# Experts of two tiles in the two halves of the array, keys ahead of exponentials, sums on VectorE

## The chip, the cores and the metric

The kernel runs on one core of one Trainium2 chip. The metric is the device time of one execution in microseconds (us). The engines of a core work side by side and meet at semaphores: TensorE (PE, matrix products; PEld is its loading of weights), VectorE (DVE), ScalarE (ACT), GpSimd (POOL) and SyncE (SP), whose queue issues the DMA transfers. Sums of matrix products land in PSUM, everything else of a tile lies in SBUF. All numbers of this kernel are float32.

## The reference

One decoder layer on x of 32 x 64 rows of 512 numbers (2048 rows), with three residual additions:

```
x = x + attention(layernorm(x))                    # 32 heads of 128, biases, RMS norm of q and k, softmax
x = x + cross_attention(layernorm(x), ctx)         # blocks of 64 rows of x against 64 rows of ctx
x = x + experts(layernorm(x))
```

The cross-attention takes, for each of the 32 blocks, x as a 64 x 512 matrix (64 channels): `q = Wq x`, `k = Wk ctx`, `v = Wv ctx`, `energy = q^T k / 8`, a softmax over the 128 columns of ctx, and `Wskip x + v attention^T`.

The experts are a router with bias vectors only:

```
logits  = x @ router_weight.T + router_bias        # 64 experts
scores  = softmax(logits)
w, idx  = top_k(scores, 8)
w_dense = zeros(2048, 64) with w at idx
out     = x * sum(w) + w_dense @ expert_bias       # expert_bias: 64 x 512
```

So what an expert adds to a row is its weight times a bias row: the mixture `w_dense @ expert_bias` is a product whose contraction is only 64 long.

## The kernel before

The 2048 rows are 16 tiles of 128 rows, taken as 8 pairs (`NPAIR`, L25). The attention proper fills the span up to about 1380 us; the change touches nothing there. What follows is the output stage.

**Products.** For each pair of tiles the attention's result (`a`, loaded by `load_mixed`, L818) is multiplied with the output weights. Pair 0 uses `plain_out` (L850 and on, with `chunks`, L832, as the inner loop). Pairs 1 to 7 use `strassen_out` (L884): a Strassen scheme of seven products of half size, `product(i, a)` at L904, each from 16 float32 products of 128x128 by 128x256 (L837), with sums and differences of blocks of `a` (128 x 2048) between them: L961, L962, L968, L975 in pairs 1 to 6, L920, L921, L922, L925 in pair 7, which has its own order of products (2, 1, 6, 5, 3, 4, 7). Pairs 1 to 6 take 2, 4, 1, 5, 7, 6, 3. L957, L960, L989 and others add a product to the residual x, which `load_residual` brought in (L176 load, L825 adds the output bias).

**Tails beside the products.** `chunks` yields after every four products (L845), so a pair of seven products has 28 steps, and after each of them the main loop (L1436 to L1438) calls `advance()`, which moves the tails of the pair before by one step. A tail is what remains of a tile after the attention: `after_attention` (L1105) runs `cross_attention` (L994) and then `experts` (L1060). `yield n` in a tail means that it sits out n steps and goes on in the one after. The second tile of a pair starts three steps after the first one (L1107). The steps on PE of a tail are the keys and values `kv` (L1003, L1004), the energies `e` (L1013, in the two row halves of the array), the turned probabilities `pt_x` (L249), the result `py_x` (L1048, L1050), the turned normalised rows `pt_f` (L249), the router `pl` (L1069), the turned weights `pw` (L1096), and the mixture `pm` (L1101). Between them stand the layernorm on DVE and POOL (L225, L226, L229, L230, L239), `kvs` copied by ACT (L1007), the softmax (L1024 maxima and L1026 on DVE, eight exponentials L1030 on ACT, L1039 and L1040 on DVE), the top-8 on DVE (L1075 to L1093), and the output (L1102 adds the mixture, L1103 stores the tile by SP).

For the mixture the weights of a tile are put into the first 64 columns of a 128-column tile whose rest is zero (`wds`, L1420), turned by PE, and multiplied with a bias table whose rows 64 to 127 are zero (`eb_sb`, L1419 to L1423). The tail of the first tile of a pair ends in step 27, that of the second one in the next pair's product 2.

**What sets the order.** PE executes in the order of the program text. The instructions of DVE, ACT and POOL in the output stage are ordered by a tile scheduler when the kernel is built (the order by hand ends at `ordered.close()`, L1399). SP issues DMAs in order. PSUM buffers come from three pools: `ps_a` with three buffers (`py`, `py_x`, `pm`), `ps_t` with two (`pt`, `pw`) and `ps_s` with three (`kv`, `e`, `pl`). The residual tiles x come from `xpool` with four buffers: x of a pair takes the buffers of the pair two before it, so its load waits for that tile's output to have been stored. The last pair's tiles (14 and 15) run their tails with no products of a further pair beside them.

Of the kernel before, what the change touches and what calls it, by code (L numbers as in the profile page):

```python
# [8 lines left out]
F32 = mybir.dt.float32  # L9
AF = mybir.ActivationFunctionType  # L10
ALU = mybir.AluOpType
AX = mybir.AxisListType

P = 128
NB, SEQ, D = 32, 64, 512
NT = NB * SEQ // P
# [12 lines left out]
NEXP = 64  # L29
# [12 lines left out]
def decoder_layer(  # L42
# [23 lines left out]
    nc = tc.nc  # L66
# [9 lines left out]
    ps_a = ctx.enter_context(tc.tile_pool(name="ps_a", bufs=3, space=bass.MemoryType.PSUM))  # L76
# [138 lines left out]
    def load(to, what):  # L215

        tc.keep_in_program_order(nc.sync.dma_start(out=to, in_=what))
# [666 lines left out]
    def strassen_out(pair, right, done, a12=None):  # L884


        ta, tb = 2 * pair, 2 * pair + 1

        def beside(what):
            return work.tile([P, BLK], F32, tag=what[:3], name=f"{what}_{pair}")  # L890

        if a12 is None:
            a12 = load_mixed(ta, 1, beside("a12"))
            a22 = load_mixed(tb, 1, block(f"a22_{pair}"))
        else:
            a22 = load_mixed(tb, 1, beside("a12"))
        a11 = load_mixed(ta, 0, beside("a11"))
        a21 = load_mixed(
            tb, 0, work.tile([P, BLK], F32, tag="a21", name=f"a21_{pair}", bufs=1)
        )  # L900
        xa, xb = load_residual(ta), load_residual(tb)
        la, ra, lb, rb_ = (xt[:, bass.ts(n, DH)] for xt in (xa, xb) for n in range(2))

        def product(i, a):  # L904
            py = out_block(f"{i}_{pair}")
            yield from chunks(py, [(a, right[i])])
            return py

        def part(what):
            return work.tile([P, DH], F32, tag=what, name=f"{what}_{pair}", bufs=1)  # L910

        def add(to, what):
            nc.gpsimd.tensor_tensor(to, to, what, ALU.add)

        if pair == NPAIR - 1:

            s1, s2 = (
                beside(what).rearrange("p (g n) -> p g n", n=P) for what in ("a12_s1", "a11_s2")
            )
            nc.vector.tensor_tensor(s1, a21, a22, ALU.add)  # L920
            nc.vector.tensor_tensor(s2, s1, a11, ALU.subtract)  # L921
            nc.gpsimd.tensor_tensor(a21, a11, a21, ALU.subtract)  # L922
            py = yield from product(2, a12)
            nc.vector.tensor_tensor(la, la, py, ALU.add)
            nc.vector.tensor_tensor(a12, a12, s2, ALU.subtract)  # L925
            yield
            py = yield from product(1, a11)
            p1 = part("p1")
            nc.scalar.copy(p1, py)
            add(la, p1)  # L930
            yield
            py = yield from product(6, s2)
            nc.vector.tensor_tensor(p1, py, p1, ALU.add)
            add(ra, p1)
            add(lb, p1)
            add(rb_, p1)
            yield
            py = yield from product(5, s1)
            p5 = part("p5")
            nc.scalar.copy(p5, py)  # L940
            add(ra, p5)
            add(rb_, p5)
            yield
            py = yield from product(3, a12)
            nc.vector.tensor_tensor(ra, ra, py, ALU.add)
            done(ta, xa)
            yield
            py = yield from product(4, a22)
            nc.vector.tensor_tensor(lb, lb, py, ALU.add)
            yield  # L950
            py = yield from product(7, a21)
            nc.vector.tensor_tensor(lb, lb, py, ALU.add)
            nc.vector.tensor_tensor(rb_, rb_, py, ALU.add)
            done(tb, xb)
            return
        py = yield from product(2, a12)
        nc.vector.tensor_tensor(la, la, py, ALU.add)  # L957
        yield
        py = yield from product(4, a22)
        nc.vector.tensor_tensor(lb, lb, py, ALU.add)  # L960
        nc.gpsimd.tensor_tensor(a22, a21, a22, ALU.add)  # L961
        nc.gpsimd.tensor_tensor(a21, a11, a21, ALU.subtract)  # L962
        yield
        py = yield from product(1, a11)
        p1 = part("p1")
        nc.scalar.copy(p1, py)
        add(la, p1)
        nc.vector.tensor_tensor(a11, a22, a11, ALU.subtract)  # L968
        yield
        py = yield from product(5, a22)  # L970
        p5 = part("p5")
        nc.scalar.copy(p5, py)
        add(ra, p5)
        add(rb_, p5)
        nc.vector.tensor_tensor(a12, a12, a11, ALU.subtract)  # L975
        yield
        py = yield from product(7, a21)
        p17 = part("p17")
        nc.vector.tensor_tensor(p17, py, p1, ALU.add)
        yield  # L980
        py = yield from product(6, a11)
        nc.vector.tensor_tensor(p1, py, p1, ALU.add)
        nc.vector.tensor_tensor(p17, py, p17, ALU.add)
        add(ra, p1)
        add(lb, p17)
        add(rb_, p17)
        yield
        py = yield from product(3, a12)
        nc.vector.tensor_tensor(ra, ra, py, ALU.add)  # L989
        yield  # L990
        done(ta, xa)
        done(tb, xb)

    def cross_attention(t, xt):  # L994


        name = f"x{t}"
# [7 lines left out]

        kvs = work.tile([P, 2, MCTX], F32, tag="kvs", name=f"kvs_{t}")
        nc.scalar.copy(kvs, kv)  # L1007
        yield 1
        halves = [slice(b * SEQ, (b + 1) * SEQ) for b in range(2)]
        e = [ps_s.tile([P, 4, MCTX], F32, tag="ps", name=f"e{b}_{name}") for b in range(2)]  # L1010
        for c in range(4):
# [45 lines left out]
            )  # L1057
        nc.vector.tensor_tensor(xt, xt, py, ALU.add)

    def experts(t, xt):  # L1060
        name = f"f{t}"
        xn = layernorm(xt, name)
        yield 4
        ft = work.tile([P, KC, P], F32, tag="ft", name=f"ft_{name}", bufs=1)
        nc.scalar.copy(ft, transposed(xn.rearrange("p (kc k) -> p kc k", k=P), name))
        yield 1
        pl = ps_s.tile([P, NEXP], F32, tag="ps", name=f"pl_{name}")
        for kc in range(KC):
            nc.tensor.matmul(  # L1069
                pl, ft[:, kc, :], rwt[:, kc, :], start=kc == 0, stop=kc == KC - 1  # L1070
            )
        lg = work.tile([P, NEXP], F32, tag="lg", name=f"lg_{name}")
        nc.vector.tensor_tensor(lg, pl, rb_b, ALU.add)
        top = small.tile([P, 8], F32, tag="top", name=f"top_{name}")
        nc.vector.max(top, lg)  # L1075
        neg = small.tile([P, 1], F32, tag="neg", name=f"neg_{name}")
        nc.vector.tensor_scalar(neg, top[:, 0:1], -1.0, None, ALU.mult)
        ex = work.tile([P, NEXP], F32, tag="ex", name=f"ex_{name}")
        den = small.tile([P, 1], F32, tag="den", name=f"den_{name}")
        nc.scalar.activation(ex, lg, AF.Exp, bias=neg, accum_out=den)  # L1080
        inv = small.tile([P, 1], F32, tag="inv1", name=f"inv1_{name}")
        nc.vector.reciprocal(inv, den)

        rest = work.tile([P, NEXP], F32, tag="rest", name=f"rest_{name}")
        nc.vector.match_replace(rest, top, lg, -3e38)
        chosen = work.tile([P, NEXP], F32, tag="chosen", name=f"chosen_{name}")
        nc.vector.tensor_tensor(chosen, lg, rest, ALU.not_equal)
        wd = wds[:, t % 2, 0:NEXP]
        nc.vector.scalar_tensor_tensor(wd, ex, inv, chosen, ALU.mult, ALU.mult)
        ws = small.tile([P, 1], F32, tag="ws", name=f"ws_{name}")  # L1090
        nc.vector.tensor_reduce(ws, wd, AX.X, ALU.add)

        nc.vector.scalar_tensor_tensor(xt, xn, ws, xt, ALU.mult, ALU.add)  # L1093
        yield 4
        pw = ps_t.tile([P, P], F32, tag="pt", name=f"pw_{name}")
        nc.tensor.transpose(pw, wds[:, t % 2, :], ident)  # L1096
        wt = work.tile([P, P], F32, tag="wt", name=f"wt_{name}")
        nc.scalar.copy(wt, pw)
        yield 1
        pm = ps_a.tile([P, D], F32, tag="pa", name=f"pm_{name}")  # L1100
        nc.tensor.matmul(pm, wt, eb_sb, start=True, stop=True)  # L1101
        nc.vector.tensor_tensor(xt, xt, pm, ALU.add)  # L1102
        nc.sync.dma_start(out=out_flat[bass.ts(t, P), :], in_=xt)  # L1103

    def after_attention(t, xt):  # L1105
        if t % 2 and t < NT - 1:
            yield 2  # L1107
        yield from cross_attention(t, xt)
        yield from experts(t, xt)


# [305 lines left out]
    load(rb_b, rb.partition_broadcast(P))  # L1417

    eb_sb = work.tile([P, D], F32, tag="eb", name="eb_sb", bufs=1)  # L1419
    wds = work.tile([P, 2, P], F32, tag="wds", name="wds", bufs=1)  # L1420
    nc.gpsimd.memset(eb_sb[NEXP:P, :], 0.0)
    nc.gpsimd.memset(wds, 0.0)
    load(eb_sb[0:NEXP, :], eb)  # L1423
    for _ in range(4):
        next(outs[1])

# [65 lines left out]
```

## Time and profile before

| what | us |
|---|---|
| median of 3 runs | 1933.31 (1930.85 to 1934.56) |
| the profiled execution's own time | 1932.7 |
| its span | 1930.9 |
| PE busy | 1887.6 (98%) |
| DVE busy | 1228.4 (64%) |
| POOL busy | 1044.3 (54%) |
| ACT busy | 646.8 (33%) |
| granted TensorE clock, mean | 0.993 |

How to read it: the span is from the first to the last instruction that the profiler saw; the execution's own time lies 1.8 us above it. Busy times of different engines overlap. A row of the timeline has the start in us from the span's beginning, the time to the last end of the merged instructions, engine, line, operation, what is written and read, the count, and in brackets how long the engine stood idle ahead of it and what released it. A row of the groups has the count after x, then total busy us and mean ns of one, then the idle time before them and its releasers. Idle time counts only on the engine that sets the end. Matmuls are pipelined, so a group's mean duration is longer than the distance between two starts.

### The profile page before, as it was taken

The numbers are of one execution on the slowest core, as the hardware profiler recorded it, in microseconds if no ns is written. First come the engines' busy times: TensorE is split into PE (matmuls) and PEld (weight loads), VectorE is DVE, ScalarE is ACT, GpSimd is POOL, SyncE is SP. The second block draws the span as 40 slices with busy tenths as digits, with TensorE's granted clock in tenths as the row PEclk, the third lists the DMA queues.
The fourth block names the chain that finished last, engine by engine and source line by source line (L and its number), as shares of the span: only waits on it lengthen the run. The fifth ranks groups of instructions, "written<-read, shape, count | busy, mean of one in ns | idle before, by whom it ended". The sixth has DMA issues, their size and how long they took to land.

```text
span 1930.9 us, 40526 instructions
## 1 busy us (share of the span) xinstructions
PE 1887.6 (98%) x16877; PEld 1622.2 (84%) x16877; DVE 1228.4 (64%) x2024; ACT 646.8 (33%) x1579; POOL 1044.3 (54%) x812
## 2 busy tenths in 40 slices
PE   9999999999999999999999999999998999999997
PEld 8888888888888888888888888888886888888874
DVE  7867777676667659666666666666454545554554
ACT  2343344344333443344333434433311202221122
POOL 5856666665667539665666666565234323332320
PEclk9999999999999999999999999999998999999998
DMA  4244334334433343334433333444932231223100
GB/s 138 67 134 142 121 126 129 110 105 131 133 111 110 107 140 107 99 101 131 133 110 111 110 100 100 130 134 137 301 127 86 90 111 67 71 88 112 49 20 23
DMA packets 164568, 214.92 MB, mean 111 GB/s; under 512 B 10144, under 2 KB 135136, under 8 KB 160288
## 3 DMA queue, kind: packets, MB, share of 16 engines
q1 hardware_dynamic: 163200, 211.24, 34.1%
q8 instruction: 133, 2.18, 0.5%
q10 hardware_dynamic: 1184, 1.08, 0.2%
q14 instruction: 51, 0.42, 0.1%
HBM read 171.92 MB, written 40.37 MB: 110 GB/s over the span
## 4 chain that ended last, share of the span: by engine, by line
PE 76%; DVE 12%; POOL 7%; issue 3%; DMA 1%; ACT 1%; SPq 0%; POOLq 0%; DVEq 0%; ACTq 0%
PE p_w L655 24%; PE py L837 19%; PE va L387 7%; PE vb L387 6%; POOL qk L734 5%; PE ms_w L779 3%; PE s L555 3%; PE o L592 3%; DVE qk L666 3%; DVE qk L679 3%; DVE qk L544 1%; PE pt_p L249 1%; PE pa L445 1%; DVE sums L262 1%; PE py_x L1050 1%
## 5 line engine op out<-in xcount | busy, mean ns | idle before, releaser
L655 PE MATMUL p_w<-x,w 128*128 128x256 f32 x2940 | 723.9, 383 | 8.6 <-DVE qk L666 8.0
L655 PEld LDWEIGHTS p_w<-x,w 128*128 128x128 f32 x2940 | 521.2, 190 | 70.7 <-DVE qk L666 13.1
L666 DVE TENSOR_TENSOR qk<-p_w,qk 128x512 f32<-128x512 f32 x360 | 213.0, 600 | 135.0 <-PE p_w L655 99.1
L356 ACT ACTIVATE sq<-qk 128x512 f32<-128x512 f32 x256 | 158.1, 629 | 400.2 <-POOL qk L734 225.4
L387 PEld LDWEIGHTS va<-w,x 128*128 128x128 f32 x2048 | 263.6, 191 | 30.5 <-ACT v L403 20.6
L387 PE MATMUL va<-w,x 128*128 128x128 f32 x2048 | 276.1, 278 | 2.1 <-ACT v L403 2.1
L837 PE MATMUL py<-wo,a 128*128 128x256 f32 x1152 | 262.5, 381 | 0.0
L679 DVE TENSOR_TENSOR qk<-p_w,qk 128x512 f32<-128x512 f32 x360 | 220.1, 620 | 57.4 <-PE p_w L655 53.9
L120 POOL TENSOR_TENSOR w<-w 128x768 f32<-128x768 f32 x126 | 244.5, 1951 | 2.4
L837 PEld LDWEIGHTS py<-wo,a 128*128 128x128 f32 x1152 | 213.9, 190 | 35.6 <-issue 7.3
L265 POOL TENSOR_TENSOR prob<-prob,inv 128x512 f32<-128x512 f32 x64 | 75.3, 1177 | 294.9 <-DVE inv L264 291.7
L542 POOL TENSOR_TENSOR qk<-qk,rs 128x512 f32<-128x512 f32 x128 | 172.4, 1347 | 113.1 <-DMA rs<-row_w 92.9
L387 PEld LDWEIGHTS vb<-w,x 128*128 128x128 f32 x1536 | 201.4, 192 | 9.7
L387 PE MATMUL vb<-w,x 128*128 128x128 f32 x1536 | 202.4, 275 | 0.0
L403 ACT COPY v<-va 128x256 f32<-128x256 f32 x256 | 94.8, 370 | 308.9 <-PE va L387 308.7
L544 DVE SCALAR_TENSOR_TENSOR qk<-qk,gqk,rs 128x512 f32<-128x512 f32 x128 | 173.4, 1355 | 11.1 <-DMA rs<-row_w 10.0
L837 PE MATMUL py<-wo_t,a 128*128 128x256 f32 x608 | 144.3, 389 | 0.0
L837 PEld LDWEIGHTS py<-wo_t,a 128*128 128x128 f32 x608 | 116.1, 195 | 16.9 <-issue 0.8
L734 POOL TENSOR_TENSOR qk<-qk 128x512 f32<-128x512 f32 x60 | 90.7, 1511 | 61.1 <-DVE qk L679 58.7
L257 DVE TENSOR_REDUCE mx<-s 128x8 f32<-128x512 f32 x64 | 44.1, 689 | 106.8 <-PE s L555 106.8
L407 DVE TENSOR_TENSOR v<-vb,v 128x256 f32<-128x256 f32 x192 | 80.8, 421 | 45.6 <-PE vb L387 27.0
L607 ACT ACTIVATE ot<-o,bvt 128x256 f32<-128x256 f32 x256 | 99.2, 469 | 2.2 <-PE o L592 2.2
(182 smaller groups left out, 2198.2 us busy)
## 6 DMA issues: line engine op xcount, KB each, us to landing
rs<-row_w SPq DMA_DIRECT2D x120, 512.0 KB
mixed<-ot SPq DMA_DIRECT2D x64, 512.0 KB
a<-mixed SPq DMA_DIRECT2D x32, 1024.0 KB
w<-in_wq_dram SPq DMA_DIRECT2D x64, 256.0 KB
w<-in_wk_dram SPq DMA_DIRECT2D x62, 256.0 KB
w<-in_wv_dram SPq DMA_DIRECT2D x62, 256.0 KB
wo<-in_wo_dram SPq DMA_DIRECT2D x8, 1024.0 KB
x<-in_x_dram SPq DMA_DIRECT2D x20, 256.0 KB
```

What stands on the lines that cost most here:

```text
L120: on.tensor_tensor(*(it.rearrange("p c j d -> p (c j) d") for it in (out, a, b)), ALU.subtract)
L356: nc.scalar.activation(sq, of, AF.Square)
L387: nc.tensor.matmul(to[:, j, :], left[i][:, c, j, :], right[i][:, c, 2, :], start=first and j == 0 and c == 0, stop=c == 1, skip_group_chec ...
L403: nc.scalar.copy(self.v[h, ab], what)
L542: nc.gpsimd.tensor_tensor(k, k, rk, ALU.mult)
L544: lambda: nc.vector.scalar_tensor_tensor(q, q, gqk, rq, ALU.mult, ALU.mult)
L607: nc.scalar.activation(ot[:, h, :, b * SEQ : (b + 1) * SEQ], o[b][:, h, :, :], AF.Identity, bias=bvt[:, hg * HG + h : hg * HG + h + 1],)
L655: nc.tensor.matmul(bank[:, s, :], self.w.inner[o][i], inner_x[self.half, o][i], start=first and s == 0, stop=True, skip_group_check=True,)
L666: nc.vector.tensor_tensor(to(t, j), bank, add(t, j), ALU.add)
L679: nc.vector.tensor_tensor(to(t, j), bank, to(t, j), ALU.add)
L734: on.tensor_tensor(qk[to], qk[to], qk[what], ALU.add)
L837: nc.tensor.matmul(py, a[:, g, :], b[g // KH][:, g % KH, :], start=n == 0 and g == 0, stop=n == last and g == NHG - 1,)
```

## The change

Three things are changed.

**Experts.** The weights of both tiles of a pair go into one tile `wds` of 128 columns, 64 for each. The first tile's `experts` ends after its top-8 and leaves its weights and its x in `chosen_by`; the second tile's takes them up, turns both tiles' weights at once, and makes two mixture products, each of 64 rows: rows 0 to 63 for the first tile, 64 to 127 for the second. The bias table lies in both halves of `eb_sb`, loaded twice, and the two zero fills are gone. Both adds and both stores follow there, in the second tile's last step. Tiles 14 and 15 (`alone`) each keep a turn and a product of their own, over 64 rows. The last `yield 4` of `experts` and its first one become `yield 3`.

**Keys.** The second tile of a pair starts its tail one step after the first one's instead of three (`yield 0` in place of `yield 2`), and four steps instead of two lie from its keys to its energies (`apart`). In the built program its copy of keys and values (L1007 before) stands on ACT ahead of the first tile's eight exponentials; before, it stood behind them.

**Sums.** L961 and L962 (pairs 1 to 6) and L922 (pair 7), differences and sums of 128 x 2048 numbers, go from POOL to DVE; L962 also moves behind a `yield`.

```diff
@@ strassen_out, pair 7
-            nc.gpsimd.tensor_tensor(a21, a11, a21, ALU.subtract)
+            nc.vector.tensor_tensor(a21, a11, a21, ALU.subtract)
@@ strassen_out, pairs 1 to 6
         py = yield from product(4, a22)
         nc.vector.tensor_tensor(lb, lb, py, ALU.add)
-        nc.gpsimd.tensor_tensor(a22, a21, a22, ALU.add)
-        nc.gpsimd.tensor_tensor(a21, a11, a21, ALU.subtract)
+        nc.vector.tensor_tensor(a22, a21, a22, ALU.add)
         yield
+        nc.vector.tensor_tensor(a21, a11, a21, ALU.subtract)
         py = yield from product(1, a11)
@@ cross_attention
-    def cross_attention(t, xt):
+    def cross_attention(t, xt, apart):
...
         nc.scalar.copy(kvs, kv)
-        yield 1
+        yield apart
@@ experts
+    chosen_by = {}
+
     def experts(t, xt):
         name = f"f{t}"
         xn = layernorm(xt, name)
-        yield 4
+        yield 3
...
-        wd = wds[:, t % 2, 0:NEXP]
+        alone = t >= NT - 2
+        side = 0 if alone else t % 2
+        if side:
+            wds, other = chosen_by.pop(t - 1)
+        else:
+            wds = work.tile([P, 2, NEXP], F32, tag="wds", name=f"wds_{name}")
+        wd = wds[:, side, :]
...
-        yield 4
+        if not alone and not side:
+            chosen_by[t] = wds, xt
+            return
+        yield 3
+        n = NEXP if alone else 2 * NEXP
         pw = ps_t.tile([P, P], F32, tag="pt", name=f"pw_{name}")
-        nc.tensor.transpose(pw, wds[:, t % 2, :], ident)
+        nc.tensor.transpose(pw[0:n, :], wds.rearrange("p a e -> p (a e)")[:, 0:n], ident)
         wt = work.tile([P, P], F32, tag="wt", name=f"wt_{name}")
-        nc.scalar.copy(wt, pw)
+        nc.scalar.copy(wt[0:n, :], pw[0:n, :])
         yield 1
-        pm = ps_a.tile([P, D], F32, tag="pa", name=f"pm_{name}")
-        nc.tensor.matmul(pm, wt, eb_sb, start=True, stop=True)
-        nc.vector.tensor_tensor(xt, xt, pm, ALU.add)
-        nc.sync.dma_start(out=out_flat[bass.ts(t, P), :], in_=xt)
+        both = [(t, xt)] if alone else [(t - 1, other), (t, xt)]
+        pms = [ps_a.tile([P, D], F32, tag="pa", name=f"pm{i}_{name}") for i in range(len(both))]
+        for i, pm in enumerate(pms):
+            rows = slice(i * NEXP, (i + 1) * NEXP)
+            nc.tensor.matmul(pm, wt[rows, :], eb_sb[rows, :], start=True, stop=True)
+        for (at, it), pm in zip(both, pms):
+            nc.vector.tensor_tensor(it, it, pm, ALU.add)
+            nc.sync.dma_start(out=out_flat[bass.ts(at, P), :], in_=it)
@@ after_attention
-        if t % 2 and t < NT - 1:
-            yield 2
-        yield from cross_attention(t, xt)
+        second = t % 2 and t < NT - 1
+        if second:
+            yield 0
+        yield from cross_attention(t, xt, 3 if second else 1)
         yield from experts(t, xt)
@@ setup of the output stage
-    wds = work.tile([P, 2, P], F32, tag="wds", name="wds", bufs=1)
-    nc.gpsimd.memset(eb_sb[NEXP:P, :], 0.0)
-    nc.gpsimd.memset(wds, 0.0)
-    load(eb_sb[0:NEXP, :], eb)
+    for half in range(2):
+        load(eb_sb[half * NEXP : (half + 1) * NEXP, :], eb)
```

In the changed kernel's lines, the mixture's add of L1102 stands at L1121, and the store of L1103 behind it.

## The prediction

> **What bounds the kernel now.** First the page's busy shares and its row of granted clock, then the busy time by stretch of the output stage, which is all that the change touches, then the order in time where TensorE (PE) stands still.
>
> ```profile
> PE 1887.6 (98%) x16877; PEld 1622.2 (84%) x16877; DVE 1228.4 (64%) x2024; ACT 646.8 (33%) x1579; POOL 1044.3 (54%) x812
> ...
> PEclk9999999999999999999999999999998999999998
> ```
> PE works 98% of the span, so only shorter PE work or one of its 43 us of idle time can pay. The clock falls in two slices, around 1450 and at the very end.
>
> ```profile
> 1450.80:1538.30 87.50, 80.36 (x409) 65.52 (x408) 39.48 (x78) 15.88 (x68) 27.72 (x24) 0.94 0.28 94
> ...
> 1645.26:1707.52 62.26, 62.26 (x324) 51.33 (x323) 32.11 (x61) 11.81 (x48) 18.99 (x18) 1.00 0.26 87
> ...
> 1832.04:1895.90 63.86, 60.36 (x328) 49.99 (x327) 33.90 (x69) 14.60 (x64) 15.02 (x19) 1.00 0.06 20
> 1895.90:1930.90 35.00, 20.88 (x85) 10.98 (x83) 16.57 (x45) 8.35 (x30) 2.71 (x6) 0.77 0.08 30
> ```
> Columns: length, then busy time of PE, weight loads, VectorE (DVE), ScalarE (ACT), GpSimd (POOL), granted clock, DMA share, GB/s. A middle pair (1645 to 1707, pairs 3 to 6 are alike) has no PE gap at all, DVE half idle: there only PE instructions count. Pair 1 (first row), pair 7 (third) and the end have gaps.
>
> ```profile
> 1479.41 0.41 ACT L1007 COPY kvs<-kv 128x256 f32<-128x256 f32 x1
> ...
> 1479.88 1.16 PE L1013 MATMUL e_x<-kvs,xn_x 64*128 64x128 f32 x16 [1.71 <-ACT kvs L1007]
> ...
> 1480.97 5.41 PE L837 MATMUL py<-wo_t,a 128*128 128x256 f32 x16
> ...
> 1831.58 4.51 POOL L922 TENSOR_TENSOR a<-a,a 128x2048 f32<-128x2048 f32 x1 [8.14 <-PE pw_f L1096]
> ...
> 1831.97 6.28 DVE L921 TENSOR_TENSOR a_s<-a_s,a 128x2048 f32<-128x2048 f32 x1
> ...
> 1841.21 1.16 PE L1013 MATMUL e_x<-kvs,xn_x 64*128 64x128 f32 x16 [1.58 <-DVE xn_x L239]
> ...
> 1850.12 1.16 PE L1013 MATMUL e_x<-kvs,xn_x 64*128 64x128 f32 x16 [1.92 <-ACT kvs L1007]
> ```
> Two gaps (1.71 and 1.92) have one cause: tile B's key copy stands on ACT behind tile A's eight exponentials. The third (1.58) is A's layernorm, held on DVE by L921, which took 6.28 us while POOL's L922 ran beside it.
>
> **The change, part by part.** I call T0 the start of a pair's product 2; A and B are the two tiles of the pair before, whose tails run beside the products.
>
> *Keys ahead.* B's key product goes one step behind A's and its ACT copy ahead of A's exponentials, so both key waits go: 1.71 in pair 1 and 1.92 in pair 7. After the first gap the 16 records of 1480.97 last 5.41 us; at full rate 16 take 3.62 (the same row kind at 1844.58), so half rate cost about 1.7 more. The Trainium skill ("TensorE: Matmul & The Clock Gate", Part 1) says that PE drops to half rate when a window of about 3.4 us ends largely idle, and that the window runs free. The row is 1.71 us of gap followed by half rate, while 1.58 and 1.92 were followed by none. By the rule alone a short gap is luck and nothing more than 1.71 is sure; by the row 3.4 comes back. I take the row: with the gap gone there is nothing to trip on. Pair 1: 3.4 (1.7 to 3.4).
>
> *Sums on VectorE.* L961, L962 and L922 leave POOL:
>
> ```profile
> L961 POOL TENSOR_TENSOR a<-a,a 128x2048 f32<-128x2048 f32 x4 | 18.2, 4552 | 12.7 <-PE py L837 12.7
> L962 POOL TENSOR_TENSOR a<-a,a 128x2048 f32<-128x2048 f32 x4 | 18.1, 4527 | 0.3
> L1101 PE MATMUL pm_f<-eb_sb,wt_f 128*128 128x512 f32 x28 | 16.2, 664 | 0.4 <-ACT wt_f L1098 0.4
> ...
> L975 DVE TENSOR_TENSOR a<-a,a 128x2048 f32<-128x2048 f32 x4 | 9.2, 2292 | 0.1
> ```
> On DVE each costs 2.29, so 4.6 more per pair against some 30 idle: nothing in pairs 1 to 6, covered by that idle time. Product 5 needs L961 at T0+25.7 and it is done near 21.9; were that cover gone, each us late would be one us of PE. In pair 7 DVE carries L920, L921, L922 in a row, 6.9, without POOL beside it, against 2.28 + 6.28 before; A's normalised x comes near T0+11.4 (both mixture adds now stand ahead of it too), PE is ready near 10.9. So the 1.58 gap shrinks to about 0.6, and product 1 waits 0.3 for its buffer. Pair 7: 1.58 + 1.92 − 0.9 = 2.6 (1.0 to 3.5).
>
> *Experts side by side.* Per pair one transpose instead of two (0.11 on PE), and two mixture products of 64 rows in the two row halves instead of two of 128. A full one holds PE for 0.86 (it begins at 1647.93 in that pair, the next product at 1648.79), so 1.72 a pair. No half-array product of 512 columns is in the trace; the nearest is L1013: 16 records of 64 rows, begun in pairs a few ns apart, hold PE for 1.09, where 16 in a row at the same 0.107 would be 1.71. That is eight pairs at 0.107, plus 0.2 for entering and leaving. Upper bound: no overlap, 1.72. Lower: full overlap, 0.86. I take 0.86 + 0.19 = 1.05, by that row. Saved: 0.67 + 0.11 = 0.78 a pair. The rule that speaks against it: the skill's "TensorEngine Tiling (Array Packing)", Gotcha 1, says that different row tiles cannot use one PSUM bank at the same time. In the built program the two results lie in different buffers for pairs 3 to 7, but pair 2's (tiles 0 and 1) get the same one, so the second product waits for VectorE's add of the first (L1121 after, L1102 before), itself behind A's maxima: 0.86 + 1.0 wait + 0.86 + 0.19 for the mode, less 0.11, against 1.72. By the row alone pair 2 would gain 0.78; by the rule it loses 1.1. I take the loss. So 5 × 0.78 − 1.1 = 2.8 (between 5 × 0.11 − 1.1 and 4.7).
> The bias table is loaded twice: one more 128 KB issue on SP (0.33) and two memsets fewer on POOL, at nothing, since PE has four steps of product 2 in that time.
>
> *What is late next.* Both outputs now leave behind the mixture step of product 2, and A's add stands on DVE behind both layernorms. The next x of this buffer waits for the output:
>
> ```profile
> 1643.82 0.34 SPq L1103 DMA_DIRECT2D out_dram<-x  x1
> 1647.59 0.33 SPq L176 DMA_DIRECT2D x<-in_x_dram  x1
> ```
>
> ```profile
> 1650.43 1.27 POOL L825 TENSOR_TENSOR x<-x,bo_b 128x512 f32<-128x512 f32 x1 [3.97 <-DMA x<-in_x_dram]
> ```
>
> ```profile
> 1651.73 0.42 DVE L957 TENSOR_TENSOR x<-x,py 128x256 f32<-128x256 f32 x1 [2.05 <-POOL x L825]
> ...
> 1653.98 1.29 DVE L1024 TENSOR_REDUCE mx_x<-e_x 128x4 f32<-128x512 f32 x2 [1.83 <-PE e_x L1013]
> ```
> Before, the output goes at T0+1.1 (T0 is 1642.75 here), the load is issued 3.77 later, its bias begins 2.84 after that, L957 ends at T0+9.4. After: layernorms to 4.9, A's add to 5.6, output issued at 5.65, load 2.1 to 3.77 later (both spacings occur), bias done at 11.9 to 13.5, L957 at 12.3 to 13.9. On DVE, A's maxima are queued behind L957; ACT's exponentials wait for them, and B's second score tile takes the buffer of A's first. From maxima to the first four exponentials done are 3.0 us, so the buffer is free at 15.3 to 16.9, and PE wants it at 16.86 (1659.6 here). Cover: 0 to 1.6 us. I charge 0.2 for each of pairs 3 to 6 (0 to 0.5): 0.8.
>
> *End.* Tiles 14 and 15 keep their own products, now half-array ones. The last mixture of pair 7's first tile moves out from between two products of tile 15's chain (about 1.0 there at half clock), and one add of 0.69 moves ahead of tile 15's layernorm: 0.3 saved, ±1 for the clock.
>
> **Sum**: 3.4 + 2.6 + 2.8 − 0.8 + 0.3 = 8.3. The profiled execution's own time is 1932.7 (span 1930.9, 1.8 around it), so 1924.4; it lies 0.6 below the median of the runs, so the forecast is 1925.0.
>
> **Rivals.**
> 1. *Late x (slower).* L957 holds A's maxima, and PE stalls before B's scores in each of pairs 3 to 6. It begins when L957 ends past T0+13.9. For: the cover is near nothing at the long spacing, two loads and two outputs now stand close on SP, and a gap can bring half rate (1.7). Against: SP and DVE are more idle than not, and the short spacing leaves 1.6. At 2 us late with half rate, 3.7 × 4 = 14.8 in place of 0.8: a loss of 5.7, 1939. It cancels all gain at 2.3 us per pair.
> 2. *No overlap in the halves.* L1013's pairs speak against it; for it, that the longest row seen so is 128 columns. The products stay at 1.72: 5 × 0.67 less, gain 5.0, 1928.3.
> 3. *The waits only move.* PE is ahead at the same places for another reason (B's layernorm on DVE, half rate from an earlier gap at 1458, the longer sums in pair 7), pairs 1 and 7 give 2 instead of 6: with the overlap as forecast 1929 to 1930, with more stalls 1932. For: 43 us of gaps have several waits ending together. Against: in the gaps named the next waiter is over 1 us earlier.
>
> **How the numbers follow.** What this kernel's measurement can tell from no change is about 0.2%, 3.9 us: faster means below 1929.4, slower above 1937.2. Chances: forecast 0.55 (1922 to 1928), no overlap 0.12 (faster), waits move 0.18 (0.14 of it within 0.2%), late x 0.15 (0.13 slower, the rest within). Faster 0.71, same 0.16, slower 0.13. The range for 8 in 10 is 1920 to 1937: below, stalls of nothing and a better end; above, the late x at half its price.
>
> **What would show it.** Right: the L1013 gaps of 1.71 and 1.92 gone, full rate after 1481; the mixture pair at about 1.05 in pairs 3 to 7 with starts together; pair 2's second one behind L1121; middle pairs near 61.7. Wrong: gaps before L1013 in each middle pair with L957 ending past T0+13.9 (rival 1), mixture records in a row (rival 2), the same gaps with another releaser (rival 3).

## The result, and the profile after

The changed kernel takes 1929.04 us (median of 17 runs, 1922.98 to 1933.23) against 1932.56 of the kernel before (17 runs, 1929.33 to 1934.56). The ratio is 0.9984, 95% interval 0.9976 to 0.9992: faster by 0.16%, by the ratio 3.1 us (1.5 to 4.6); the medians lie 3.5 apart. The forecast was 1925.0, 8.3 below the median known then. The time lies in the stated range, but the gain is 3.1 where 8.3 was forecast.

The page of the changed kernel, busy shares and granted clock:

```profile
PE 1886.2 (98%) x16870; PEld 1618.9 (84%) x16870; DVE 1221.7 (63%) x2037; ACT 645.7 (33%) x1572; POOL 999.8 (52%) x797
...
PEclk9999999999999999999999999999999999999997
```

PE works 1.4 less and DVE 6.7 less. In the row of the clock the 8 around 1450 is now a 9, and the last slice has 7 where it had 8.

By stretch, the output stage's setup with pair 1 and part of pair 2, a middle pair, pair 7, and the end (columns as in the prediction; the first stretch ends later than the one shown there, so those two are not to be subtracted):

```profile
1449.58:1539.09 89.51, 83.28 (x419) 67.31 (x418) 42.53 (x79) 15.71 (x67) 19.29 (x23) 0.94 0.29 96
...
1706.56:1768.25 61.69, 61.69 (x323) 50.73 (x322) 30.56 (x62) 11.65 (x47) 12.19 (x17) 1.00 0.26 88
1829.94:1891.30 61.36, 60.72 (x330) 50.46 (x329) 31.89 (x71) 14.91 (x64) 13.02 (x18) 1.00 0.07 20
1891.30:1929.10 37.80, 22.38 (x85) 11.77 (x83) 16.36 (x45) 7.99 (x29) 2.70 (x6) 0.65 0.07 28
```

A middle pair is 0.57 shorter and still without a gap. DVE works less there (30.6 instead of 32.1), though it has two sums more. The end is the only one of these rows whose clock is lower than before (0.65, against 0.77).

In order of time, the places where PE waited before, and three where it waits now (L1121 is the mixture's add, L1102 before):

```profile
1471.30 0.37 ACT L1008 COPY kvs<-kv 128x256 f32<-128x256 f32 x1 [1.86 <-PE kv L1005]
...
1479.34 1.16 PE L1014 MATMUL e_x<-kvs,xn_x 64*128 64x128 f32 x16
...
1529.58 1.12 PE L1119 MATMUL pm_f<-eb_sb,wt_f 64*128 64x512 f32 x2 [0.78 <-DVE x L1121]
...
1530.64 5.41 PE L837 MATMUL py<-wo_t,a 128*128 128x256 f32 x16
...
1845.53 1.16 PE L1014 MATMUL e_x<-kvs,xn_x 64*128 64x128 f32 x14 [0.64 <-ACT prob_x L1031]
...
1893.45 0.69 DVE L225 BATCH_NORM_STATS2 st_x<-x 128x6 f32<-128x512 f32 x1
...
1894.05 0.67 DVE L1121 TENSOR_TENSOR x<-x,pm_f 128x512 f32<-128x512 f32 x1
1894.64 0.18 DVE L226 BATCH_NORM_AGGREGATE mv_x<-st_x 128x2 f32<-128x6 f32 x1
...
1896.51 1.16 PE L1014 MATMUL e_x<-kvs,xn_x 64*128 64x128 f32 x16 [2.22 <-DVE xn_x L239]
```

At the end before, one of the two adds came behind the layernorm (L239), at 1900.16:

```profile
1900.16 0.68 DVE L1102 TENSOR_TENSOR x<-x,pm_f 128x512 f32<-128x512 f32 x1
...
1900.39 1.16 PE L1013 MATMUL e_x<-kvs,xn_x 64*128 64x128 f32 x16 [0.81 <-DVE xn_x L239]
```

The key copy (1471.30) is done early, and the energies at 1479.34 follow without a wait. In pair 2 the second mixture product waits 0.78 for VectorE's add of the first, and the 16 records behind it take 5.41 instead of 3.72. (A record is one entry of PE in the trace; a product leaves two, a turn one.) At the end, an add of a finished tile stands between the two statistics steps of tile 15's layernorm, and the energies wait 2.22 instead of 0.81.

The costs by line, a middle pair's mixture, and the residual's way in a middle pair:

```profile
L1041 DVE TENSOR_TENSOR prob_x<-prob_x,inv_x 128x512 f32<-128x512 f32 x24 | 16.6, 691 | 1.0
...
L1119 PE MATMUL pm_f<-eb_sb,wt_f 64*128 64x512 f32 x28 | 10.9, 712 | 0.7 <-ACT wt_f L1112 0.7
...
L961 DVE TENSOR_TENSOR a<-a,a 128x2048 f32<-128x2048 f32 x4 | 9.1, 2284 | 0.0
...
L1027 DVE TENSOR_SCALAR neg_x<-mx_x 128x4 f32<-128x4 f32 x24 | 3.4, 158 | 0.0
```

```profile
1705.51 1.13 PE L1119 MATMUL pm_f<-eb_sb,wt_f 64*128 64x512 f32 x4
```

```profile
1708.98 0.94 SPq L1122 DMA_DIRECT2D out_dram<-x  x2
1711.08 0.96 SPq L176 DMA_DIRECT2D x<-in_x_dram  x2
...
1713.82 2.49 POOL L825 TENSOR_TENSOR x<-x,bo_b 128x512 f32<-128x512 f32 x2 [6.08 <-DMA x<-in_x_dram]
...
1715.12 0.42 DVE L957 TENSOR_TENSOR x<-x,py 128x256 f32<-128x256 f32 x1 [5.61 <-POOL x L825]
...
1718.75 0.18 DVE L1040 RECIPROCAL inv_x<-sums_x 128x4 f32<-128x4 f32 x1 [1.50 <-ACT prob_x L1031]
...
1721.03 1.16 PE L1014 MATMUL e_x<-kvs,xn_x 64*128 64x128 f32 x16
```

The mixture's products have 64 rows now, and in a middle pair the four records of both tiles lie within 1.13. The sum of L961 takes 2.28 on DVE as costed, and L1041 (before: L1040, 1245 ns) takes 691. The first four exponentials are done at 1718.75, 2.3 before PE wants their buffer at 1721.03: late x does not reach PE.

To see where the time went I divided the span at starts that both kernels have: the first key product, the first turned probability of each pair's first tile (pt_x), and tile 15's energies. The entries are us longer (+) or shorter than in the profile of before, so each row sums to the difference of the spans.

| profile | up to the keys | pair 1 | pair 2 | pairs 3 to 6 | pair 7 | to tile 15's energies | from there to the end | sum |
|---|---|---|---|---|---|---|---|---|
| changed kernel | +1.25 | −3.5 | +3.0 | −2.3 | −3.1 | +0.7 | +2.1 | −1.8 |
| the same again | −0.6 | −3.5 | +1.3 | −2.3 | −3.1 | +0.7 | −1.3 | −8.7 |
| keys alone | +1.7 | −3.3 | 0 | 0 | −1.1 | 0 | −0.5 | −3.2 |
| sums alone | +2.5 | −3.5 | 0 | 0 | −0.7 | 0 | 0 | −1.7 |
| experts alone | 0 | −1.7 | +1.3 | −1.2 | +2.4 | +0.7 | +1.2 | +2.8 |
| keys and sums | +0.15 | −3.5 | 0 | 0 | −3.6 | 0 | −2.1 | −9.1 |
| own bank in pair 2 | 0 | −3.5 | −0.6 | −2.3 | −3.1 | +0.7 | +0.2 | −8.5 |
| full array | +0.75 | −3.5 | +1.0 | −0.4 | −3.1 | +0.5 | −1.2 | −5.9 |
| adds later at the end | +2.0 | −3.5 | +1.3 | −2.3 | −2.9 | −0.6 | +0.6 | −5.2 |
| both repairs | +0.6 | −3.5 | −0.6 | −2.3 | −3.0 | −0.6 | +0.9 | −8.5 |

The first column lies mostly in the attention, which no kernel changes; it is scatter, and so is much of the last (shown below). The middle ones mostly repeat to 0.1 from profile to profile of what is the same there. The exception is pair 2 of the changed kernel, +3.0 and +1.3: the 1.7 between them is half rate, which only the first profile has. "Experts alone" loses a further 1.0 between the two tiles of pair 2, which the table puts under pairs 3 to 6. Times, where given, are medians with their own runs of before.

### The profile page after: what moved, and what is told of

Its sections match the earlier page's. It is cut to its first block, busy times and chain, and to the rows that moved or that the text cites. A ratio compares the mean times of both kernels' runs of the same rounds, so it can differ in the third digit from the quotient of the medians.

```text
span 1929.1 us, 40470 instructions
## 1 busy us (share of the span) xinstructions
PE 1886.2 (98%) x16870; PEld 1618.9 (84%) x16870; DVE 1221.7 (63%) x2037; ACT 645.7 (33%) x1572; POOL 999.8 (52%) x797
## 4 chain that ended last, share of the span: by engine, by line
PE 76%; DVE 12%; POOL 7%; issue 3%; DMA 1%; ACT 0%; SPq 0%; POOLq 0%; DVEq 0%; ACTq 0%
PE p_w L655 25%; PE py L837 19%; PE va L387 7%; PE vb L387 6%; POOL qk L734 5%; PE ms_w L779 3%; PE o L592 3%; PE s L555 3%; DVE qk L666 3%; DVE qk L679 3%; DVE qk L544 1%; PE pt_p L249 1%; PE pa L445 1%; DVE sums L262 1%; PE py_x L1051 1%
## 5 line engine op out<-in xcount | busy, mean ns | idle before, releaser
L544 DVE SCALAR_TENSOR_TENSOR qk<-qk,gqk,rs 128x512 f32<-128x512 f32 x128 | 176.5, 1379 | 11.4 <-DMA rs<-row_w 10.7
L913 POOL TENSOR_TENSOR x<-x,p 128x256 f32<-128x256 f32 x42 | 42.8, 1038 | 180.7 <-ACT p L966 84.2
```

Of the source, the lines that this page charges most:

```text
L544: lambda: nc.vector.scalar_tensor_tensor(q, q, gqk, rq, ALU.mult, ALU.mult)
```

## The experiments

**Keys alone.** The kernel before, with

```diff
-            yield 2
-        yield from cross_attention(t, xt)
+            yield 0
+        yield from cross_attention(t, xt, 3 if second else 1)
```
(and the 3 in place of the 1 behind the key copy).

> The kernel before with the key part alone: the second tile starts one step after the first, its keys four steps ahead of its energies; the sums stay on POOL and the experts stay apart. If the waits at the key copy were what the change wins, pair 1 loses its gap of 1.71 and the half rate behind it (1.7) and pair 7 its gap of 1.92, while pair 7's gap of 1.58 behind L921 stays: 5.3 us faster than before, about 0.9973. The rival, that these waits only move to the next waiter (the exponentials, slowed by POOL's sums, hold the score buffers), gives less than 2 us.

Measured: 1928.62 (11 runs), ratio 0.9981 (0.9973 to 0.9990). Pair 1's gap is gone, 3.3 as expected. Pair 7 gave 1.1, not 1.9, since the next waiter was close:

```profile
1839.57 1.16 PE L1013 MATMUL e_x<-kvs,xn_x 64*128 64x128 f32 x16 [1.15 <-DVE xn_x L239]
...
1847.41 0.83 PE L1013 MATMUL e_x<-kvs,xn_x 64*128 64x128 f32 x10 [0.89 <-ACT prob_x L1030]
```
The second one now waits for exponentials, which the DVE queue behind L921 held. The first gap shrank a little too (1.58 to 1.15). Of the 1.5 that the two lost, 1.1 reached the pair's time; where the rest went is open.

**Sums alone.** The kernel before, with L961, L962 and L922 on VectorE.

> The kernel before with only the three sums of 128x2048 on VectorE. My theory: DVE is no longer slowed by POOL, so in pair 1 the exponentials come over 2 us earlier and the key copy behind them is no longer late (3.4 us), and pair 7's gap of 1.58 shrinks by about 1: 4.4 us faster, about 0.9977. The rival, that DVE's longer queue takes back what the contention gives, makes it equal to before within 1 us.

Measured: 1925.85 (10 runs), ratio 0.9968 (0.9959 to 0.9978). This is the simplest edit of the three, and its runs show the largest gain, 6.2 by the ratio against 3.7 for the keys; the two intervals overlap slightly. By the stages of their profiles the two edits are alike (4.2 and 4.4), so the order of the two is not shown. It removes pair 1's gap too, without touching the keys. The groups from 1560 us on show why, first the kernel before, then this one:

```profile
L1040 DVE TENSOR_TENSOR prob_x<-prob_x,inv_x 128x512 f32<-128x512 f32 x24 | 29.9, 1245 | 1.1
...
L1026 DVE TENSOR_SCALAR neg_x<-mx_x 128x4 f32<-128x4 f32 x24 | 14.1, 619 | 0.0
```

```profile
L1040 DVE TENSOR_TENSOR prob_x<-prob_x,inv_x 128x512 f32<-128x512 f32 x24 | 16.6, 691 | 1.0
L1026 DVE TENSOR_SCALAR neg_x<-mx_x 128x4 f32<-128x4 f32 x24 | 6.1, 272 | 0.1
```
Two small steps of the softmax take 21 us less once POOL has no such sums beside them. In pair 7 both gaps stayed, shorter (1.41 and 1.35): this alone is not enough there.

**Experts alone.** The changed kernel with keys and sums put back.

> The expert part alone (keys and sums as before). If the profile of the changed kernel is read rightly, pairs 3 to 7 gain 0.57 each (2.9 in all), pair 2 loses 3.0 (a wait of 0.8 for the one bank, half rate behind it) and the end loses about 2.8 (adds queued ahead of tile 15's layernorms, half rate): 2 to 3 us slower than before, about 1.0013. If the halves were worth what was forecast and pair 2 and the end are chance, it is 2 to 4 us faster.

Measured: 1936.14 (12 runs), ratio 1.0022 (1.0011 to 1.0032): slower, as expected (1.0013) and a little more. Pair 7 was not expected: 2.4 longer. Its rows, and those of pair 1:

```profile
1479.92 1.16 PE L1014 MATMUL e_x<-kvs,xn_x 64*128 64x128 f32 x16 [1.72 <-ACT kvs L1008]
1481.01 5.23 PE L837 MATMUL py<-wo_t,a 128*128 128x256 f32 x23
...
1830.40 6.28 DVE L921 TENSOR_TENSOR a_s<-a_s,a 128x2048 f32<-128x2048 f32 x1
...
1836.60 1.27 DVE L1121 TENSOR_TENSOR x<-x,pm_f 128x512 f32<-128x512 f32 x2
...
1837.33 1.99 PE L837 MATMUL py<-wo,a 128*128 128x256 f32 x8 [1.57 <-DVE x L1121]
...
1849.49 2.08 PE L1014 MATMUL e_x<-kvs,xn_x 64*128 64x128 f32 x16 [2.85 <-ACT kvs L1008]
```
Both mixture adds stand behind the slow L921, and PE's next product waits for their bank. The key copy is later too: the three gaps of this pair (1.57, 0.33 and 2.85) are 1.25 longer than the two of before, and half rate follows the last one (the 16 records of 1849.49 take 2.08 instead of 1.16). So the expert part leans on the other two: in the changed kernel, with L921 at 2.28 and the keys ahead, none of the three is there. In pair 1 the gap of 1.72 is there, yet the 23 records behind it run at full rate (5.23): with the same gap, the kernel before ran at half rate. The clock shows it; first the window with the gap and the next one in the kernel before, then the window with the gap here (windows set by the profile's own changes of clock):

```profile
1478.05:1481.47 3.42, 1.71 (x19) 1.45 (x19) 3.24 (x5) 2.04 (x12) 1.30 (x1) 1.00 0.00 0
1481.47:1484.88 3.41, 3.41 (x9) 2.71 (x9) 3.41 (x3) 0.00 (x0) 0.41 (x1) 0.50 0.00 0
```

```profile
1477.26:1480.67 3.41, 1.69 (x17) 1.24 (x17) 2.40 (x3) 2.88 (x16) 0.46 (x1) 1.00 0.00 0
```
PE was busy for half of the window in both, and only one was followed by half clock.

**An own bank in pair 2.**

```diff
-        pms = [ps_a.tile([P, D], F32, tag="pa", name=f"pm{i}_{name}") for i in range(len(both))]
+        pms = [
+            ps_t.tile([P, D], F32, tag="pt", name=f"pm{i}_{name}")
+            if t == 1 and i == 1
+            else ps_a.tile([P, D], F32, tag="pa", name=f"pm{i}_{name}")
+            for i in range(len(both))
+        ]
```

> The changed kernel, but in pair 2 the second mixture result goes into a bank of another pool, so that the two products lie in different banks as in pairs 3 to 7. If the shared bank costs pair 2 its wait and the half rate behind it, pair 2 goes from 3.0 slower to about 0.6 faster than before: 3.5 us faster than the changed kernel, about 0.9965 of before. If the half rate there is chance, only the wait of 0.8 and the lost overlap of 0.7 come back: 1.5 us.

Measured: 1924.68 (8 runs), ratio 0.9969 (0.9955 to 0.9982), 2.9 us below the changed kernel by the ratios, whose intervals overlap. Pair 2 goes from +3.0 to −0.6, the gain of every middle pair:

```profile
1526.49 1.13 PE L1124 MATMUL pm_f<-eb_sb,wt_f 64*128 64x512 f32 x4
1527.55 2.64 PE L837 MATMUL py<-wo_t,a 128*128 128x256 f32 x11
```
The four records now overlap, and full rate follows. In the first profile of the changed kernel the clock was halved there:

```profile
1530.68:1534.09 3.41, 3.41 (x9) 2.78 (x9) 1.07 (x2) 0.00 (x0) 0.00 (x0) 0.50 0.54 172
```

**Full array.** Each tile's turned weights in a tile of their own, whose other rows are zero; one turn and one step for both, as in the changed kernel.

```diff
-        nc.scalar.copy(wt[0:n, :], pw[0:n, :])
+        for i in range(n // NEXP):
+            rows = slice(i * NEXP, (i + 1) * NEXP)
+            nc.scalar.copy(wt2[rows, i, :], pw[rows, :])
...
-            nc.tensor.matmul(pm, wt[rows, :], eb_sb[rows, :], start=True, stop=True)
+            nc.tensor.matmul(pm, wt2[:, i, :], eb_sb, start=True, stop=True)
```

> The changed kernel with the mixture products over the full array: each tile's turned weights lie in a tile whose other 64 rows are zero, so each product takes all 128 rows and the two run one after the other; one turn and the common step stay. If the halves really overlap (1.26 a pair with entering and leaving, against 1.72), middle pairs get 0.46 longer each (62.15 instead of 61.69), 2.3 in all, and no slow step stands around the mixtures. If half mode gives nothing, the middle pairs stay at 61.7.

Measured: 1928.89 (11 runs), ratio 0.9981 (0.9972 to 0.9990), not told from the changed kernel in the whole. A middle pair and its mixture tell it:

```profile
1703.83 1.88 PE L1120 MATMUL pm_f<-eb_sb,wt 128*128 128x512 f32 x4
```

```profile
1644.52:1706.67 62.15, 62.15 (x323) 51.27 (x322) 30.75 (x64) 11.93 (x48) 12.21 (x16) 1.00 0.25 87
```
62.15 against 61.69: the halves are worth 0.46 in each of pairs 3 to 6, 1.84 in all. In pair 7 and ahead of tile 15 they gave nothing: both kernels wait there for DVE, and pair 2 is even 0.3 dearer with them.

**Adds later at the end.** The mixture adds of tiles 12 and 13 are issued behind the statistics of tile 15's first layernorm, that of tile 14 behind those of its second.

```diff
+            aggregate[0] = nc.vector.bn_aggr(mv[:, i, :], st)
...
+        behind = ExitStack()
+        if NT - 3 <= t < NT - 1:
+            yield 1
+            behind.enter_context(tc.issue_after(aggregate[0].ins))
+        with behind:
             for (at, it), pm in zip(both, pms):
                 nc.vector.tensor_tensor(it, it, pm, ALU.add)
```

> The changed kernel, but at the end the mixture adds of tiles 12 and 13 are issued on DVE behind the statistics of tile 15's first layernorm, and that of tile 14 behind those of its second. If the adds queued ahead of these layernorms are what the end lost, the gap of 2.2 before the energies falls to about 0.8 and that before tile 15's second turn comes 1.3 earlier: 2.7 us faster than the changed kernel. If the end's loss is only the clock (half rate from 1903 on), it stays within 0.5.

Measured: 1924.33 (6 runs), ratio 0.9962 (0.9948 to 0.9976). Up to tile 15's energies 1.3 came back (+0.7 to −0.6), half of the 2.7 expected. What follows them differs between profiles by more than the edit is worth, see below.

**Both repairs.**

> Both repairs: the bank of pair 2 and the adds at the end. The two stages are 370 us apart, so the gains should add: 5 to 6 us faster than the changed kernel, about 0.995 of before, 1923. If one repair only moves half rate into another stage, it is under 4.

Measured: 1921.79 (5 runs, 1920.95 to 1924.23), ratio 0.9947 (0.9935 to 0.9959), 7.1 us below the changed kernel by the ratios: more than the two stages show, and the lowest median of all. The end of the changed kernel, of its second profile, and of this one:

```profile
1896.50:1929.10 32.60, 19.40 (x66) 10.04 (x66) 13.10 (x38) 6.64 (x26) 1.91 (x4) 0.60 0.04 16
```

```profile
1893.00:1922.20 29.20, 15.84 (x66) 8.87 (x66) 13.02 (x38) 6.65 (x26) 1.92 (x4) 0.73 0.05 18
```

```profile
1891.00:1922.40 31.40, 19.40 (x66) 10.06 (x66) 13.60 (x39) 6.65 (x26) 1.92 (x4) 0.60 0.08 31
```
Two profiles of one kernel differ by 3.4 from tile 15's energies on, and their PE busy time by 3.6, for the same 66 records at a mean clock of 0.60 and 0.73: that is the rate alone. The first and the third have the same busy time and clock, and they differ by 1.2; that fits the later add of tile 14, which here stands behind the layernorm's statistics and no longer between them.

**Late x.** In pairs 3 to 6 POOL gets four more operations for each tile's x:

```diff
         xa, xb = load_residual(ta), load_residual(tb)
+        if 3 <= pair < NPAIR - 1:
+            for xt in (xa, xb):
+                for op in (ALU.subtract, ALU.add) * 2:
+                    nc.gpsimd.tensor_tensor(xt, xt, bo_b, op)
```

> The changed kernel with the residual made late on purpose: in pairs 3 to 6 the bias is subtracted and added twice more on POOL ahead of its use (four more operations of 1.27 for each tile, 5.1 us; the sum is the same). In the changed kernel the first four exponentials are done 2.3 us before PE wants their buffer. If L957 holding the maxima is the way a late x reaches PE, each of pairs 3 to 6 gets a gap of about 2.8 before the second tile's energies, with or without half rate of up to 1.7 behind it: middle pairs 64.5 to 66.2 and 11 to 18 us slower than the changed kernel. If DVE's queue does not pass it on, the middle pairs stay at 61.7.

Measured: 1968.19 (one run), 39 us above the changed kernel where 11 to 18 were expected.

```profile
1664.78 8.71 POOL L905 TENSOR_TENSOR x<-x,bo_b 128x512 f32<-128x512 f32 x7
```

```profile
1670.96 0.42 DVE L961 TENSOR_TENSOR x<-x,py 128x256 f32<-128x256 f32 x1 [14.36 <-POOL x L905]
```

```profile
1668.12 0.48 PE L1018 MATMUL e_x<-kvs,xn_x 64*128 64x128 f32 x2
1675.16 2.07 PE L1018 MATMUL e_x<-kvs,xn_x 64*128 64x128 f32 x14 [6.55 <-ACT prob_x L1035]
1677.16 5.22 PE L837 MATMUL py<-wo,a 128*128 128x256 f32 x15
```
(The add of product 2, L957 elsewhere, is L961 here.) The dose was mis-sized: POOL did both tiles' operations in turn, so the first tile's x came 8.7 late and not 5.1 (its add ends 20.1 behind T0, against 11.4 in the changed kernel; T0 is set 16.86 ahead of the second tile's energies, as in the forecast). Less the cover of 2.3 that leaves a gap of 6.4; the four gaps are 6.4 to 6.7. So the way is the one named, and the cover is what the profile gave. Each of the four pairs is 9.2 to 9.9 longer than in the changed kernel: the gap, and half rate behind it.

**Keys and sums, without the expert part.**

> Keys and sums without the expert part: does the expert part win anything as it stands? By stages: pair 1 gains its 1.7 of gap (3.4 where half rate stood behind it), pairs 2 to 6 and the end stay as before, pair 7 loses both gaps nearly (2.5 to 3.2). That is 4.2 to 6.6 us faster than before, 0.9966 to 0.9978, so not slower than the changed kernel: the 2.3 won in pairs 3 to 6 by the halves are lost again in pair 2 (1.3) and at the end (1.3 and more). If the halves' gain reached the end, this kernel is 2 us slower than the changed one.

Measured: 1924.29 (6 runs), ratio 0.9965 (0.9952 to 0.9977). **The changed kernel once more**, beside it on the same chip:

> The changed kernel once more, for a second profile of it. If half rate behind a short gap is chance, the gap of 0.78 in pair 2 comes back with its length and the 1.7 of half rate behind it probably does not (one of five profiles with this gap had it so far); the delay of tile 15's energies against the middle pairs (0.7, and 1.3 more than with the adds moved) comes back as it was. The time is that of the changed kernel, 0.9984 of before. If half rate belongs to this gap, it stands at the same place again.

Measured: 1928.45 (9 runs), ratio 0.9978 (0.9968 to 0.9988). Without the expert part the kernel is 4.2 us faster than with it (medians of one chip). Pair 7 gives 3.6 without the experts and 3.1 with them. Pair 2 of the second profile of the changed kernel:

```profile
1527.70 1.12 PE L1119 MATMUL pm_f<-eb_sb,wt_f 64*128 64x512 f32 x2 [0.78 <-DVE x L1121]
1528.75 3.72 PE L837 MATMUL py<-wo_t,a 128*128 128x256 f32 x16
```
The same gap as in the first profile, and full rate behind it: half rate does not belong to this gap each time. Of the five profiles with this gap (changed kernel twice, experts alone, adds later, late x) it stood in one.

**The clock of every run.** For each run the mean granted clock is on record, not only for the profiled ones. Runs with a mean of 0.991 or less:

| kernel | runs at 0.991 or less |
|---|---|
| before | 7 of 60 |
| keys alone, sums alone, keys and sums | 0 of 27 |
| experts alone | 10 of 12 |
| changed kernel, both times | 21 of 26 |
| full array | 6 of 11 |
| own bank in pair 2 | 3 of 8 |
| adds later at the end | 3 of 6 |
| both repairs | 0 of 5 |

Of the changed kernel's 26 runs, these 21 took 1927.06 to 1933.23 (median 1929.43), and the five at 0.993 or more took 1922.98 to 1925.43 (median 1924.35); none lies between. All six runs of keys and sums alone have 0.993 or more, and their median is 1924.29. So at the higher clock the expert part neither wins nor loses, and what it costs in most runs comes with the lower clock. The lower clock goes with its two new waits: each repair has fewer such runs, and with both there are none. A run's mean does not say where in the span the clock fell. The two profiles of the changed kernel (0.991 and 0.994) differ in pair 2 and at the end.

## Why the prediction was right and wrong

**The sum.** Without half rate behind the new waits, the stages up to tile 15's energies give 3.5 + 3.1 − 1.3 + 2.3 − 0.7 = 6.9 (second profile of the changed kernel), near the forecast. What the forecast lacked is half rate behind the waits that the change itself makes: it stood at nothing in pair 2 and within ±1 at the end. The runs at the lower clock take about 5 more (1929.43 against 1924.35), and they are 21 of 26. At 0.993 or more the kernel before takes 1931.1 (median of 38 runs on three chips), so there the gain is 6.7. That keys and sums came out so near the forecast is in part luck, as follows.

**Keys and sums: right, one half of it for the wrong reason.** Pair 1 gave 3.5 of 3.4 in the profile. But of the two prices weighed, the row's and the rule's, the row was one throw: "experts alone" has the gap and not the half rate. Of the Trainium skill's rule ("TensorE: Matmul & The Clock Gate", Part 1) one thing fits: half clock came for one window of 3.41, as long as the page's window of about 3.4 us. But the page asks for an idle window, and here gaps of 1.71 and 0.78 were followed by half clock; the measurement decides. Nor does the place of the gap within the window tell the two profiles apart, since PE was busy for 1.71 and 1.69 of it. So only the gap's 1.71 is sure, and what decides about the rest stays open. Pair 7 gave 3.1; the forecast had 2.6 and 0.78. The gap that remained, 0.64, has the size forecast (0.6) at another place: within tile 13's energies, behind the exponentials of tile 12, while tile 12's own energies no longer wait.

**"4.6 more per pair against some 30 idle": right that it is hidden, wrong in sign.** DVE's busy time in a middle pair fell by 1.5. The sum left out that POOL's sums slowed DVE's own rows (1245 to 691 ns, 619 to 158 in the changed kernel), though it used the same effect for L921. With the sums alone moved the two rows fall to 691 and 272, so most of it is the sums' doing.

**Pair 2: the loss was right.** Expected +1.1, shown +1.3, and the own bank removes it. What the trace shows is the wait for the add that reads the shared buffer (0.78 behind L1121). Whether two row halves could write one bank at the same time, which is what the prediction takes from the Trainium skill ("TensorEngine Tiling (Array Packing)", Gotcha 1), no run here shows. What the forecast missed is that a new gap brings its own chance of half rate, 1.7 in the first profile.

**Halves: right mechanism, one term too small.** Overlap is complete (all four records in 1.13), but the forecast took 0.19 for entering and leaving, and the records show 0.40: the first record begins 0.31 behind the last full one where 0.22 is usual, the two pairs of records take 0.527 and 0.519 where a full record takes 0.43, and the second full record behind them follows after 0.32. So a pair costs 1.26, not 1.05, and a middle pair gains 0.57 and not 0.78.

**"What is late next": too dear by 0.8.** The output left 4.8 behind T0 (forecast 5.65), the load came 2.1 later, L957 ended at 11.4, not 12.3 to 13.9. That this 0.8 and the halves' 0.2 a pair cancel in pairs 3 to 6 is luck.

**"End: 0.3 saved": wrong in sign.** It costs 0.7 up to tile 15's energies; putting the adds later turns that into −0.6, so the queue is the cause. That is the add of 0.69 that the forecast had charged. It had also credited 1.0 for the product that leaves tile 15's chain. But that product now comes earlier, and so does its add on DVE: tile 14's add stands between the statistics of tile 15's second layernorm, which was not in the sum and costs up to 1.2 where the mixture runs at half rate.

**The rivals.** Late x is refuted at this size, and its mechanism shown. No overlap is refuted. The measured time is the one that "the waits only move" gave (1929 to 1930), but its places are wrong: the waits named in pairs 1 and 7 went, and new ones came where the expert part moved two adds, pair 2 and the end. With keys and sums alone the gain is 6.8 by the ratio, near the forecast's 8.3 for everything; as it stands the expert part takes 2.5 to 4 of it back, and with its two new waits gone or shortened it adds 3.5 (0.9965 to 0.9947; the two intervals overlap). By the stages alone the part costs 1.3 in pair 2, 0.7 at the end and 0.5 in pair 7 and wins 2.3 in pairs 3 to 6, about even, and the runs at the higher clock agree. The rest of those 2.5 to 4 comes with the lower clock of most of its runs. How much of it falls in pair 2 and how much at the end stays open.

## What to carry to other kernels

When a step is put together with its neighbour, list for each place in the program (first pair, middle, last, and the end with nothing beside it) which bank each result gets and what stands ahead of its reader; a saving of 0.6 per pair was lost at the two places that differ. Before buying PE time with a reordering, look for slowed rows on the engine that feeds it: large sums moved from POOL to an already busier DVE made DVE's total fall in a middle pair, and by the medians won most of what there was. A stretch of half rate seen once behind a short gap is not a fixed price, and a new short gap is not free of it either: compare the granted clock over many runs, not over two profiles.

## What had not been expected of the hardware

- In the profiles, half rate behind short gaps came now and then, behind long ones always: it followed pair 1's gap of 1.7 in one of two profiles, pair 2's of 0.78 in one of five, none of six gaps of 1.15 to 1.92 in pair 7, and gaps of 6.4 to 6.7 in four of four.
- With waits of 0.78 in pair 2 and 2.2 at the end, 21 of 26 runs had a mean clock of 0.991 or less. With the first gone and the second at 0.9 it was none of five.
- At the end, where PE has gaps of up to 3.7, the same 66 records took 15.8 and 19.4 us of PE time in two profiles of one kernel.
- Two half-array records of 512 columns side by side take 0.52 where one full record takes 0.43, with a further 0.1 on entering and on leaving.
- A 128x4 scaling on DVE took 619 ns on average in the kernel with the sums of 128x2048 on POOL (153 to 2394), and 158 in the changed kernel.
